# Left and right kept by pairs of channels: TensorE reads right in place at a step of 16 bytes

## Chip, cores and metric

One core of a Trainium2 chip. The metric is the device time of one execution in microseconds (us). All data are f32.

## What is computed

`x` has 384 x 384 positions of 128 channels. The first layer multiplies triangles of positions, the second gates each row:

```
z = layernorm(x)
left  = (z @ Wl + bl) * sigmoid(z @ Wlg + blg)
right = (z @ Wr + br) * sigmoid(z @ Wrg + brg)
core = einsum('bikh,bjkh->bijh', left, right)
zo = layernorm(core) @ Wout + bout
x = x + sigmoid(x @ Wg + bg) * zo
...
out = (x @ W_left + b_left + x @ W_eq + b_eq) * sum_j(x @ W_right + b_right)
out = (out * sigmoid(x @ W_gate + b_gate)) @ W_out + b_out
y = layernorm(out + x) * ln_scale + ln_bias
```

The change concerns `left`, `right` and the `einsum`: for each of the 128 channels h, a 384 x 384 by 384 x 384 product, with k summed.

## The kernel before

There are 128 partitions, and N = 384 is cut into NB = 3 blocks of 128. Each engine's instructions run in the order in which the program writes them (`seq` keeps it); the work of the stages was interleaved by hand.

**Stage 1** makes left and right. Its 144 chunks (kb, ig, c) each hold 128 positions k and XR = 8 positions i. Per position i one matmul (L372) takes the 128 x 128 columns of the normalised x as weights and `wz`, 512 columns wide, as the moving operand: left and right alternate in the first 256 results, their gates follow. For the first PLAIN = 8 chunks the weights are contiguous columns in the tile `stage`; for the rest they are taken from `columns[n][:, q, :, i]` (tile `xc`), where neighbouring columns are four f32, 16 bytes, apart. ACT makes the sigmoid (L383), DVE the product (L385), which goes to the tile `lr`, [k, h, i, s], s = 0 for left and 1 for right. So the two sides of one channel are neighbours, and a channel's G = 64 positions are a run of 512 bytes. Full `lr` tiles are stored to `lr_d` in HBM in slices of 16 channels (L357, one after each step). The last KEEP = 2 of the 18 tiles stay in SBUF (`kept`).

**Stage 2** computes core, one channel h at a time. `load_h` (L85, DMAs at L92, on SP's queue) brings left and right of a channel into `lrh`, [k, kb, i, s], in runs of 512 bytes, three channels ahead. `fill` (L576) runs on POOL: it copies the kept pieces in (L586 for left, L587 for right) and copies right out of `lrh` into the contiguous tile `rr` (L592, L593), a channel ahead. Then nine matmuls (L611), three kb by three row blocks ib, take left from `lrh` as weights, at a step of 8 bytes, and `rr` as the moving operand, 384 contiguous columns. ACT moves the result to `ct` (L620) and squares it into `sq` (L621), DVE adds both up (L622, L623), and the channel goes to `core_d` (L627), on SP's queue behind `load_h(h + 3)`.

**Stage 3** takes the variance and its root from the sums (L527 to L559; tiles `ve`, `r`, `m` of the pool `rstd`) and runs the rest row by row: L721 to L851.

Tile pools set how far each side can run ahead: two `lr` tiles, three `lrh`, two `rr`, two `ct`, one `sq`.

Of the kernel before, what the change touches and what calls it, by code (L numbers as in the profile page):

```python
# [8 lines left out]
F32 = mybir.dt.float32  # L9
# [5 lines left out]
P = 128  # L15
# [4 lines left out]
def triangle_then_gated_row_kernel(ctx: ExitStack, tc: tile.TileContext, a: dict, out: bass.AP):  # L20
# [13 lines left out]
    nc = tc.nc  # L34
    x_nat, x_tok, x_row = a["x_nat"], a["x_tok"], a["x_row"]
    NG8, C = x_nat.shape[1], x_tok.shape[2]
    N = 8 * NG8
    H = a["L0_side_b"].shape[0] // 4
    assert C == P and H == P and N % P == 0
    NB = N // P  # L40
    G = 64
    NG = N // G
    XR = 8
    KEEP = 2
# [3 lines left out]

    cpool = ctx.enter_context(tc.tile_pool(name="const", bufs=1))
    dpool = ctx.enter_context(tc.tile_pool(name="scratch", bufs=1, space=DRAM))  # L50
    lr_d = dpool.tile([NB * NG, P, H, 2 * G], F32, name="lr_d")
    core_d = dpool.tile([N, H, N], F32, name="core_d")
    rstd_d = dpool.tile([N, N], F32, name="rstd_d")
    nd_d = dpool.tile([NB * NG8, 8 * P], F32, name="nd_d")
# [1 line left out]
    def seq(ins):  # L56

        return tc.keep_in_program_order(ins)
# [19 lines left out]
    kept = {(NB - 1, ig): None for ig in range(NG - KEEP, NG)}  # L78
    end2 = ctx.enter_context(ExitStack())
    with ExitStack() as ctx2:  # L80
        lrp = ctx2.enter_context(tc.tile_pool(name="lr", bufs=2))
        inp = [ctx2.enter_context(tc.tile_pool(name="p2in", bufs=2))]
        loaded2 = {}

        def load_h(h):  # L85

            if h < H:
                t = inp[h % 3 // 2].tile([P, NB, N, 2], F32, tag="lrh", name="lrh")
                src = lr_d[:, :, h].rearrange("g p e -> p g e")
                dst = t.rearrange("p b (g i) s -> p (b g) (i s)", i=G)  # L90
                for g in slice(0, NG), slice(NG, NB * NG - KEEP):
                    seq(nc.sync.dma_start(out=dst[:, g], in_=src[:, g]))  # L92
                loaded2[h] = t

        with tc.tile_pool(name="p1w", bufs=5, side="right") as wp, \
# [6 lines left out]
            NQ = XR // 4  # L104
            AHEAD, LEAD = 4, 15
            FETCH = 6
            HS = H // 8
            loaded, normed = {}, {}
            lr, full = {}, []
            batches, at = [(n, n + 1) for n in range(PLAIN)], PLAIN  # L110
# [28 lines left out]
                seq(nc.sync.dma_start(out=t[0:1], in_=nd_d[n:n + 1, 4 * P * q:4 * P * (q + 1)]))  # L139


            stage = lrp.tile([P, H, G, 2], F32, tag="lr", name="stage").rearrange("p h i s -> p (h i s)")
            load_chunk(0, slice(0, 4))

            wst, g0, b0 = stage[:, 0:4 * H], stage[:, 4 * H:4 * H + 1], stage[:, 4 * H + 1:4 * H + 2]
# [207 lines left out]
            def store_slice():  # L353

                if full:
                    kb, ig, hs, t = full.pop(0)
                    seq(nc.sync.dma_start(  # L357
                        out=lr_d[kb * NG + ig, :, hs:hs + HS].rearrange("k h e -> k (h e)"),
                        in_=t[:, hs:hs + HS].rearrange("k h i s -> k (h i s)"),
                    ))  # L360

            def back(n, q, half, between=None):


                kb, ig, c = chunks[n]
                if c == 0 and q == 0 and half == 0:
                    lr[kb, ig] = lrp.tile([P, H, G, 2], F32, tag="lr", name="lr")
                t = lr[kb, ig]
                pr = pps.tile([P, 2, 4 * H], F32, tag="pr", name="pr")
                for r in range(2):  # L370
                    i = 2 * half + r
                    seq(nc.tensor.matmul(  # L372
                        pr[:, r, :], lhsT=columns[n][:, 4 * q + i, :] if n < PLAIN else columns[n][:, q, :, i],
                        rhs=wz, start=True, stop=True,
                    ))
                    if r == 0 and between:
                        between()
                r0 = 4 * q + 2 * half
                own, c0 = normed[n]
                rs = [terms[own][3][:, c0 + r:c0 + r + 1] for r in range(r0, r0 + 2)]  # L380
                sg = [wp.tile([P, 2 * H], F32, tag="sg", name="sg") for _ in range(2)]
                for r in range(2):
                    seq(nc.scalar.activation(sg[r], pr[:, r, 2 * H:], AF.Sigmoid, scale=rs[r]))  # L383
                for r in range(2):
                    seq(nc.vector.scalar_tensor_tensor(  # L385
                        t[:, :, c * XR + r0 + r, :],
                        pr[:, r, :2 * H].rearrange("k (h s) -> k h s", s=2),
                        rs[r],
                        sg[r].rearrange("k (h s) -> k h s", s=2),
                        ALU.mult, ALU.mult,  # L390
                    ))
                if c == G // XR - 1 and q == NQ - 1 and half == 1:
                    if (kb, ig) in kept:
                        kept[kb, ig] = t
                    else:
                        full.extend((kb, ig, hs, t) for hs in range(0, H, HS))

            steps = [(n, q) for n in range(len(chunks)) for q in range(NQ)]
            fetch = {0: [4, 5], 1: [6, 7]}
# [45 lines left out]
            for n in range(PLAIN, len(chunks)):  # L445
                k = 2 + (n - PLAIN) // 2
# [12 lines left out]
            for k, (n, q) in enumerate(steps):  # L459
# [4 lines left out]
                if k > 0:  # L464
                    more = 4 if k in (6, len(steps) - 6) else 1
# [47 lines left out]
                    late_products(m2)  # L513
                if k == len(steps) - 2 * G // 4 + 16:
                    assert not full
                    for h in range(2):
                        load_h(h)


        spool, rp = (end2.enter_context(tc.tile_pool(name=n, bufs=b, side="right", reuse_waits="tile"))  # L520
                     for n, b in (("stats", 1), ("rstd", 2)))
        roots = {}


# [1 line left out]

        def variance(b, s):  # L527
            if b not in roots:
                roots[b] = [rp.tile([P, N], F32, tag=n, name=n, bufs=c) for n, c in (("ve", NB), ("r", NB), ("m", 2))]
            ve, _, m = (w[:, s] for w in roots[b])  # L530
            if b > 0:
                seq(nc.scalar.activation(m, csum[:, b, s], AF.Square, scale=1.0 / H))
                seq(nc.scalar.activation(ve, csq[:, b, s], AF.Copy, scale=1.0 / H))
                seq(nc.gpsimd.tensor_tensor(ve, ve, m, ALU.subtract))
                seq(nc.gpsimd.tensor_scalar(ve, ve, 0.0, EPS, ALU.max, ALU.add))
                return
            seq(nc.vector.scalar_tensor_tensor(m, csum[:, b, s], 1.0 / (H * H), csum[:, b, s], ALU.mult, ALU.mult))
            seq(nc.vector.scalar_tensor_tensor(ve, csq[:, b, s], 1.0 / H, m, ALU.mult, ALU.subtract))
            seq(nc.vector.tensor_scalar(ve, ve, 0.0, EPS, ALU.max, ALU.add))
# [18 lines left out]
            seq(nc.vector.scalar_tensor_tensor(r, r, -0.5, ve, ALU.mult, ALU.mult))  # L558
            seq(nc.vector.scalar_tensor_tensor(r, r, 1.5, m, ALU.add, ALU.mult))  # L559

        with tc.tile_pool(name="p2r", bufs=2, side="right", reuse_waits="tile") as rrp, \
             tc.tile_pool(name="p2more", bufs=1, side="right", reuse_waits="tile") as more, \
             tc.tile_pool(name="p2out", bufs=2, side="right", reuse_waits="tile") as op, \
             tc.tile_pool(name="p2sq", bufs=1, side="right", reuse_waits="tile") as qp, \
             tc.tile_pool(name="p2ps", bufs=2, space=PSUM, reuse_waits="tile") as ps, \
             tc.tile_pool(name="p2one", bufs=1, space=PSUM, reuse_waits="tile") as ps1:
            csum = spool.tile([P, NB, N], F32, name="csum")
# [2 lines left out]
            seq(nc.vector.memset(csq, 0.0))  # L570

            inp.append(more)
            load_h(2)
            right = {}

            def fill(h):  # L576

                if h < H:
                    t = loaded2[h]
                    rr = right[h] = rrp.tile([P, NB, N], F32, tag="rr", name="rr")  # L580
                    i1 = G * (NG - KEEP)

                    def stay():
                        for (kb, ig), lrt in kept.items():
                            i = slice(ig * G, (ig + 1) * G)
                            seq(nc.gpsimd.tensor_copy(t[:, kb, i, 0], lrt[:, h, :, 0]))  # L586
                            seq(nc.gpsimd.tensor_copy(rr[:, kb, i], lrt[:, h, :, 1]))  # L587


                    if h > 0:  # L590
                        stay()
                    seq(nc.gpsimd.tensor_copy(rr[:, :NB - 1], t[:, :NB - 1, :, 1]))  # L592
                    seq(nc.gpsimd.tensor_copy(rr[:, NB - 1, :i1], t[:, NB - 1, :i1, 1]))  # L593
                    if h == 0:
                        stay()

            fill(0)
            for h in range(H):
                fill(h + 1)
                t, rr = loaded2.pop(h), right.pop(h)  # L600
                pc = ps.tile([P, NB, 512], F32, tag="pc", name="pc")
                banks = [pc[:, ib, :N] for ib in range(NB)]
                order = [(kb, ib) for kb in range(NB) for ib in range(NB)]
# [5 lines left out]
                    seq(nc.scalar.activation(warm, mhalf[:, 0:1], AF.Sqrt, scale=-1.0))  # L609
                for kb, ib in order:  # L610
                    seq(nc.tensor.matmul(  # L611
                        banks[ib], lhsT=t[:, kb, ib * P:(ib + 1) * P, 0], rhs=rr[:, kb],
                        start=(kb == 0), stop=(kb == NB - 1),
                    ))

                ct = op.tile([P, NB, N], F32, tag="ct", name="ct")
                sq = qp.tile([P, NB, N], F32, tag="sq", name="sq")
                to = core_d[:, h, :].rearrange("(b p) j -> p b j", p=P)
                if h < H - 1:
                    seq(nc.scalar.copy(ct, pc[:, :, :N]))  # L620
                    seq(nc.scalar.activation(sq, ct, AF.Square))  # L621
                    seq(nc.vector.tensor_add(csum, csum, ct))  # L622
                    seq(nc.vector.tensor_add(csq, csq, sq))  # L623
                    load_h(h + 3)

                    queue = nc.sync if h < H - 3 else nc.scalar
                    seq(queue.dma_start(out=to, in_=ct))  # L627
# [24 lines left out]
    with ExitStack() as ctx3:  # L652
# [49 lines left out]
        i1 = 0  # L702
# [280 lines left out]
```

## Time and profile before

| | us |
|---|---|
| median of three runs (lowest to highest) | 3155.5 (3154.95 to 3156.49) |
| the profiled execution's own time | 3154.78 |
| its span in the profile | 3152.9 |
| stage 1, to the first matmul of L611 | 1010 |
| stage 2, the matmuls of L611 | 742.9 |
| stage 3 | 1400 |
| share of 16 DMA engines busy, HBM traffic over the span | 74%, 252 GB/s |

How to read it. An f32 matmul appears as two MATMUL records on PE, each with one LDWEIGHTS record on PEld, which overlaps PE: 1152 matmuls of L611 are 2304 records. A group's row gives the line, engine, operation, what it writes and reads, its shape and count, then busy us and the mean ns of one, then the engine's idle time before it and what ended it. Records of a busy PE overlap, so busy time over count, not the mean, is the pace. The chain is the work that ended last, followed back from the end. The granted clock of TensorE is 0.999 of full speed in this execution.

### The profile page before, as it was taken

The numbers are of one execution on the slowest core, as the hardware profiler recorded it, in microseconds if no ns is written. First come the engines' busy times: TensorE is split into PE (matmuls) and PEld (weight loads), VectorE is DVE, ScalarE is ACT, GpSimd is POOL, SyncE is SP. The second block draws the span as 40 slices with busy tenths as digits, with TensorE's granted clock in tenths as the row PEclk, the third lists the DMA queues.
The fourth block names the chain that finished last, engine by engine and source line by source line (L and its number), as shares of the span: only waits on it lengthen the run. The fifth ranks groups of instructions, "written<-read, shape, count | busy, mean of one in ns | idle before, by whom it ended". The sixth has DMA issues, their size and how long they took to land.

```text
span 3152.9 us, 44536 instructions
## 1 busy us (share of the span) xinstructions
PE 3135.5 (99%) x11306; PEld 2132.8 (68%) x11306; DVE 2473.6 (78%) x7409; ACT 1808.5 (57%) x3755; POOL 2392.9 (76%) x3066
## 2 busy tenths in 40 slices
PE   9999999999999999999999999999999999999998
PEld 4777777777776666666666666677777777777776
DVE  8888888888885555555555788888888888888998
ACT  4444444444444343343433577777777777777777
POOL 6888888888886656666566587788888888888887
PEclk9999999999999999999999999999999999999999
DMA  4978878788883999999999865666666666666562
GB/s 154 340 302 304 326 279 340 281 320 299 312 304 106 282 282 283 282 284 282 284 282 283 298 231 202 220 224 221 219 220 218 221 220 219 220 220 222 210 213 109
DMA packets 509102, 797.42 MB, mean 253 GB/s; under 512 B 56689, under 2 KB 419569, under 8 KB 492466
## 3 DMA queue, kind: packets, MB, share of 16 engines
q1 hardware_dynamic: 507552, 792.61, 74.0%
q8 instruction: 94, 1.54, 0.2%
q10 hardware_dynamic: 1234, 1.77, 0.2%
q14 instruction: 158, 1.29, 0.1%
q0 software_dynamic: 64, 0.20, 0.0%
HBM read 508.14 MB, written 286.36 MB: 252 GB/s over the span
## 4 chain that ended last, share of the span: by engine, by line
PE 98%; DVE 1%; ACT 0%; issue 0%; DMA 0%; POOL 0%; POOLq 0%; DVEq 0%; ACTq 0%
PE pr L372 31%; PE pc L611 23%; PE py L781 8%; PE pr L752 8%; PE pg L769 8%; PE pl L770 8%; PE pg L721 8%; PE py L782 4%; DMA core_d<-ct 0%; PE pt L335 0%; PE pq L729 0%; ACT py L816 0%; PE pb L740 0%; POOL rs L286 0%; DVE m L547 0%
## 5 line engine op out<-in xcount | busy, mean ns | idle before, releaser
L372 PE MATMUL pr<-wz,xc 128*128 128x512 f32 x2176 | 935.1, 592 | 0.0
L372 PEld LDWEIGHTS pr<-wz,xc 128*128 128x128 f32 x2176 | 670.5, 308 | 263.9 <-POOL xc L324 1.2
L383 ACT ACTIVATE sg<-pr,rs 128x256 f32<-128x256 f32 x1152 | 483.8, 471 | 508.3 <-ACT sg L383 354.7
L611 PE MATMUL pc<-rr,lrh 128*128 128x384 f32 x2304 | 743.3, 486 | 0.4 <-DVE lr L385 0.4
L611 PEld LDWEIGHTS pc<-rr,lrh 128*128 128x128 f32 x2304 | 452.0, 196 | 291.8 <-issue 1.1
L385 DVE SCALAR_TENSOR_TENSOR lr<-pr,rs,sg 128x256 f32<-128x256 f32 x1152 | 501.7, 477 | 164.3 <-ACT sg L383 158.9
L816 ACT ACTIVATE py<-py,nm,rs 128x128 f32<-128x128 f32 x1149 | 493.1, 430 | 159.7 <-DVE u L774 80.6
L781 PEld LDWEIGHTS py<-wo,u 128*128 128x128 f32 x2304 | 376.6, 191 | 97.5
L622 DVE TENSOR_TENSOR csum<-csum,ct 128x1152 f32<-128x1152 f32 x127 | 175.0, 1378 | 332.9 <-ACT ct L620 332.9
L781 PE MATMUL py<-wo,u 128*128 128x128 f32 x2304 | 402.1, 275 | 0.0
L620 ACT COPY ct<-pc 128x1152 f32<-128x1152 f32 x127 | 142.3, 1120 | 445.2 <-PE pc L611 439.7
L743 POOL TENSOR_TENSOR cs<-ct,rt 128x384 f32<-128x384 f32 x380 | 379.7, 1000 | 8.3 <-DMA rt<-rstd_d 4.4
L851 POOL TENSOR_TENSOR yt<-yt,lnb 128x384 f32<-128x384 f32 x380 | 380.6, 1003 | 2.9 <-DVE yt L845 2.6
L324 POOL TENSOR_TENSOR xc<-xc,bc 128x512 f32<-128x512 f32 x272 | 345.8, 1271 | 24.0
L286 POOL TENSOR_TENSOR rs<-nd,mhalf 128x8 f32<-128x8 f32 (+1 forms) x145 | 236.3, 1630 | 146.8 <-ACT sg L383 107.2
L796 DVE BATCH_NORM_STATS2 st<-py 128x6 f32<-128x128 f32 x1152 | 266.0, 286 | 87.2 <-PE py L782 85.1
L592 POOL COPY rr<-lrh 128x768 f32<-128x768 f32 x128 | 190.8, 1490 | 167.2 <-DMA lrh<-lr_d 156.4
L782 PE MATMUL py<-ident,x1T 128*128 128x128 f32 x1152 | 314.0, 273 | 0.0
L752 PE MATMUL pr<-cs,wc 128*128 128x384 f32 x768 | 313.5, 490 | 0.0
L769 PE MATMUL pg<-x1T,mat_L_conv_W_gate 128*128 128x384 f32 x768 | 310.7, 486 | 0.9 <-ACT g L772 0.9
L721 PE MATMUL pg<-xt,mat_L_conv_Wg 128*128 128x384 f32 x768 | 310.7, 487 | 0.3 <-ACT ct L635 0.2
L770 PE MATMUL pl<-x1T,mat_L_conv_W_left 128*128 128x384 f32 x768 | 310.5, 486 | 0.0
(124 smaller groups left out, 4302.2 us busy)
## 6 DMA issues: line engine op xcount, KB each, us to landing
lr_d<-lr SPq DMA_DIRECT2D x128, 1024.0 KB
lrh<-lr_d SPq DMA_DIRECT2D x128, 640.0 KB
xt<-in_x_row_dram SPq DMA_DIRECT2D x96, 768.0 KB
ct<-core_d SPq DMA_DIRECT2D x95, 768.0 KB
rt<-rstd_d SPq DMA_DIRECT2D x95, 768.0 KB
out_dram<-yt SPq DMA_DIRECT2D x94, 768.0 KB
core_d<-ct SPq DMA_DIRECT2D x125, 576.0 KB
xt<-in_x_nat_dram SPq DMA_DIRECT2D x136, 512.0 KB
```

The lines of the kernel that those rows point to most:

```text
L372: seq(nc.tensor.matmul(pr[:, r, :], lhsT=columns[n][:, 4 * q + i, :] if n < PLAIN else columns[n][:, q, :, i], rhs=wz, start=True, stop=Tr ...
L383: seq(nc.scalar.activation(sg[r], pr[:, r, 2 * H:], AF.Sigmoid, scale=rs[r]))
L385: seq(nc.vector.scalar_tensor_tensor(t[:, :, c * XR + r0 + r, :], pr[:, r, :2 * H].rearrange("k (h s) -> k h s", s=2), rs[r], sg[r].rearra ...
L611: seq(nc.tensor.matmul(banks[ib], lhsT=t[:, kb, ib * P:(ib + 1) * P, 0], rhs=rr[:, kb], start=(kb == 0), stop=(kb == NB - 1),))
L721: seq(nc.tensor.matmul(pg[:, :N], lhsT=wg0, rhs=r["xT"], start=True, stop=True))
L752: seq(nc.tensor.matmul(pr[:, :N], lhsT=wc, rhs=r["cs"], start=True, stop=True))
L769: seq(nc.tensor.matmul(pg2[:, :N], lhsT=wgate, rhs=r["x1T"], start=True, stop=True))
L770: seq(nc.tensor.matmul(pl[:, :N], lhsT=wleft, rhs=r["x1T"], start=True, stop=True))
L781: seq(nc.tensor.matmul(py[:, s], lhsT=r["u"][:, s], rhs=r["wo"], start=True, stop=False))
L782: seq(nc.tensor.matmul(py[:, s], lhsT=r["x1T"][:, s], rhs=ident, start=False, stop=True, is_transpose=True))
L816: seq(nc.scalar.activation(py[:, s], py[:, s], AF.Identity, bias=bias, scale=scale))
L851: seq(engine.tensor_tensor(yt, yt, lnbb, ALU.add))
```

## The change

The two innermost sizes are regrouped: a tile holds pairs of channels, and for a position four values lie together, left and right of the even channel and left and right of the odd one. A pair's 64 positions are one run of 1 KB in `lr` and in `lr_d`. Loads are by pair and block kb (`load_block`) in place of by channel, with five buffers of [k, 384, 4], a pair's three loads placed after the second channel's matmuls. `fill`, `rr` and POOL's copies of right are gone: L611's successor takes both weights and moving operand from `lrh`, each at a step of four f32, 16 bytes. POOL copies only the kept pieces, four values at a time, once a pair (`fill_last`). `sq` and the tiles of the root share one tile, `arena`. The counts of matmuls, and what they compute, are as before.

```diff
-    lr_d = dpool.tile([NB * NG, P, H, 2 * G], F32, name="lr_d")
+    lr_d = dpool.tile([NB * NG, P, H // 2, 4 * G], F32, name="lr_d")
...
-        inp = [ctx2.enter_context(tc.tile_pool(name="p2in", bufs=2))]
+        inp = [ctx2.enter_context(tc.tile_pool(name="p2in", bufs=3))]
...
-        def load_h(h):
-
-            if h < H:
-                t = inp[h % 3 // 2].tile([P, NB, N, 2], F32, tag="lrh", name="lrh")
-                src = lr_d[:, :, h].rearrange("g p e -> p g e")
-                dst = t.rearrange("p b (g i) s -> p (b g) (i s)", i=G)
-                for g in slice(0, NG), slice(NG, NB * NG - KEEP):
-                    seq(nc.sync.dma_start(out=dst[:, g], in_=src[:, g]))
-                loaded2[h] = t
+        def load_block(n):
+
+            p, kb = divmod(n, NB)
+            if p < H // 2:
+                t = loaded2[p, kb] = inp[n % 5 // 3].tile([P, N, 4], F32, tag="lrh", name="lrh")
+                g = slice(kb * NG, (kb + 1) * NG - (KEEP if kb == NB - 1 else 0))
+                seq(nc.sync.dma_start(
+                    out=t.rearrange("p (g i) e -> p g (i e)", i=G)[:, :g.stop - g.start],
+                    in_=lr_d[g, :, p].rearrange("g p e -> p g e"),
+                ))
...
-                    lr[kb, ig] = lrp.tile([P, H, G, 2], F32, tag="lr", name="lr")
+                    lr[kb, ig] = lrp.tile([P, HP, G, 4], F32, tag="lr", name="lr")
...
-                        pr[:, r, :2 * H].rearrange("k (h s) -> k h s", s=2),
+                        pr[:, r, :2 * H].rearrange("k (h e) -> k h e", e=4),
...
+        arena = spool.tile([P, 2 + 2 * NB, N], F32, name="arena")
+        own_root = [[arena[:, n] for n in place] for place in ((0, 1, 2), (3, 5, 7), (4, 6, 2))]
...
-            def fill(h):
...
-                    seq(nc.gpsimd.tensor_copy(rr[:, :NB - 1], t[:, :NB - 1, :, 1]))
-                    seq(nc.gpsimd.tensor_copy(rr[:, NB - 1, :i1], t[:, NB - 1, :i1, 1]))
...
+            def fill_last(h):
+
+                if h < H and h % 2 == 0:
+                    for (kb, ig), lrt in kept.items():
+                        seq(nc.gpsimd.tensor_copy(loaded2[h // 2, kb][:, ig * G:(ig + 1) * G], lrt[:, h // 2]))
...
-                        banks[ib], lhsT=t[:, kb, ib * P:(ib + 1) * P, 0], rhs=rr[:, kb],
+                        banks[ib], lhsT=loaded2[h // 2, kb][:, ib * P:(ib + 1) * P, 2 * (h % 2)], rhs=loaded2[h // 2, kb][:, :, 2 * (h % 2) + 1],
...
+                if h % 2 == 1:
+                    for n in range(5, 5 + NB):
+                        load_block(h // 2 * NB + n)
+                fill_last(h + 1)
...
-                sq = qp.tile([P, NB, N], F32, tag="sq", name="sq")
+                sq = arena[:, 3:3 + NB]
```

## The prediction

> **What bounds the kernel now.** I read the shares and the chain of the page first, then its groups. Columns of a group: busy us, mean ns of one instruction, idle before it. A matmul in f32 is two MATMUL records with two weight loads (PEld LDWEIGHTS); I call each a pass.
>
> ```profile
> PE 3135.5 (99%) x11306; PEld 2132.8 (68%) x11306; DVE 2473.6 (78%) x7409; ACT 1808.5 (57%) x3755; POOL 2392.9 (76%) x3066
> ...
> PE 98%; DVE 1%; ACT 0%; issue 0%; DMA 0%; POOL 0%; POOLq 0%; DVEq 0%; ACTq 0%
> ...
> L372 PEld LDWEIGHTS pr<-wz,xc 128*128 128x128 f32 x2176 | 670.5, 308 | 263.9 <-POOL xc L324 1.2
> ...
> L611 PE MATMUL pc<-rr,lrh 128*128 128x384 f32 x2304 | 743.3, 486 | 0.4 <-DVE lr L385 0.4
> L611 PEld LDWEIGHTS pc<-rr,lrh 128*128 128x128 f32 x2304 | 452.0, 196 | 291.8 <-issue 1.1
> ...
> L592 POOL COPY rr<-lrh 128x768 f32<-128x768 f32 x128 | 190.8, 1490 | 167.2 <-DMA lrh<-lr_d 156.4
> ```
>
> TensorE is the bound everywhere: 99% busy, 98% of the chain. Stage 2, which the change rewrites, is the L611 row: 2304 passes in 743.3 us, 322.6 ns a pass, with 0.4 us of idle before them. (The mean of 486 ns is one pass from its start to its end; passes overlap, so I price by busy time over count.) The stretches by stage say the same: cut at the first and last pass of L611, that line alone:
>
> ```profile
> 1010.00:1752.90 742.90, 742.83 (x2304) 451.98 (x2304) 1.00 0.95 282
> ```
>
> (length, PE, PEld, granted clock, DMA share, GB/s). So a stage of 742.9 us has no PE gap to win, at full clock. Whatever POOL or the DMAs do less of there gains nothing; whatever a pass costs more counts 2304 times.
>
> The row that matters most comes from the weight loads split by form:
>
> ```profile
> L372 PEld LDWEIGHTS pr<-wz,xc 128*128 128x128 f32 x2176 | 670.5, 308 | 263.9 <-POOL xc L324 1.2 <-issue 0.7
> L611 PEld LDWEIGHTS pc<-rr,lrh 128*128 128x128 f32 x2304 | 452.0, 196 | 291.8 <-issue 1.1
> ...
> L372 PEld LDWEIGHTS pr<-wz,stage 128*128 128x128 f32 x128 | 22.9, 190 | 24.6 <-issue 19.4 <-ACT stage L336 3.5 <-ACT sg L383 1.7
> ```
>
> One instruction, 128 columns each, three steps between columns: 4 bytes (the first eight chunks, from stage) 190 ns; 8 bytes (lrh) 196 ns; 16 bytes (xc) 308 ns. The first and the last are the same line of code, with the same matmul beside them. TensorE's own read of SBUF in f32 is thus 118 ns dearer for 128 columns at 16 bytes, and nearly free at 8. Moving operands, in contrast, are all contiguous before: wz, rr, xt, cs, x1T. No row shows a strided one.
>
> Who waits in stage 2 (total us, times, longest), and the DMA line of the same stretch (the queue's packets, MB, share of 16 engines):
>
> ```profile
> ACT ct L620 <- PE pc L611: 432.7, 124, 3.5
> DVE csum L622 <- ACT ct L620: 328.0, 125, 3.4
> POOL rr L592 <- DMA lrh<-lr_d: 155.7, 123, 3.1
> POOL rr L587 <- PE pc L611: 120.7, 125, 2.1
> ...
> q1 hardware_dynamic: 310791, 204.84, 95.2%
> ```
>
> All wait for PE; but the DMA engines are 95% occupied, so loads have little room.
>
> **What the Trainium skill says.** "SBUF — State Buffer", section Door 1 (the note on cachelines): SBUF is read in lines of 16 bytes, at least two accesses must hit a line to absorb its latency, and an access that goes to a new line each time pays. It then says that 4 fp32 can be strided for free, which is just this change's 16 bytes. The trace sides with the first sentence and against the second: 308 ns against 190. "TensorE: Matmul & The Clock Gate", Part 2: weights and moving operand have two independent read ports. So the weight row is an analogy for the moving one, and not its measurement; that both run beside each other undisturbed agrees with L372, where 308 ns of load hide under a pass of 430 (935.1/2176). "DMA: Bandwidth & Descriptors", Specifications: 512 bytes are the least for full rate. Loads before are at just that, and 95% busy at 282 GB/s; nothing before shows what 1 KB gives.
>
> **The change part by part.**
> - *Right as moving operand in place, step 16 bytes.* Each of 384 columns now lies in its own line. Contiguous, a pass takes 322.6/384 = 0.84 ns a column. The weight load's extra at 16 bytes is 118 ns for 128 columns, 0.92 ns each: about one more such step a column. The moving read's price is not in the trace. So from both sides. Below: 0, if the moving port fetches a line in 0.84 ns or less. A gain is excluded: the columns are as many, and contiguous is the best case. Above: the weight row's whole extra, 118 x 3 = 354 ns a pass, x 2304 = 816 us. Between lies the plain doubling, 320 ns a pass (a second 0.833 ns step for 384 columns): 2304 x 320 = 737 us. I take 740: the remaining 11 ns of the 118 look like a start-up cost, which passes in a row would hide. All of it is on the path, since PE is the path.
> - *Left as weights, step 8 to 16 bytes:* from 196 to 308 ns, from the two rows. It lies beside the previous pass; 308 < 322 even if passes stay as they are, so 0. If that cover were short by 10 ns, 23 us; with doubled passes it has over 300 ns to spare.
> - *POOL copies removed:* 128 of L592 (1490 ns) and as many of L593, and four pieces of 64 a channel; in their place two copies of 256 elements a pair of channels. POOL was 449 of 724 us busy in stage 2 and released only matmuls that never waited: 0. Each new copy is about 0.5 us at L592's 1490/768 = 1.9 ns an element; PE's kb = 2 matmuls of the pair wait for it. It is queued behind nothing on POOL.
> - *Loads by block:* three DMAs a pair (512, 768, 768 KB) for four before, the same 2 MB, half the packets. They go out on SP after the pair's last matmuls release each buffer, so the store of core_d for the odd channel stands behind them on SP; ACT needs that ct buffer only two channels later: 0. With stage 2 doubled the traffic falls to about 282/2 = 141 GB/s, and nothing here is late.
> - *Stage 1:* L385 writes 4 in a row where it wrote 2, as many elements (477 ns, two for each 1.72 us of four passes); slices to lr_d remain 8 KB a partition: 0. First loads: 2 MB as before. *Arena:* sq and the roots share space, each still written before it is read on the same engines, at the seam where all wait for the last matmuls: 0, at most the seam's chain, 2 to 3 us (PE idles 0.3 us there now).
>
> Sum against the profiled execution: 3154.8 (span 3152.9 and 1.9 around it) + 740 = 3895. The median of the runs is 0.7 above that execution; I leave 3895.
>
> **The rivals.**
> - *A, doubled passes* (640 to 680 ns each): 3154.8 + 737 to 816 = 3892 to 3971; with some 15 us of slop, 3875 to 3985. For it: the weight row on the same engine, and the page's two-hit sentence.
> - *B, the moving port is quick enough: not slower.* Place: the L611 pass. Price: 0. It decides from a line fetch of at most 0.84 ns (322.6/384). Then 322 ns passes stay and only the seams move: 3150 to 3158. For it: separate ports, and "4 fp32" free. Against it: 308.
> - *C, B's port, but block loads are late.* The kb = 2 block is asked for when three matmuls of the odd channel are done, and used twelve matmuls later: 12 x 0.645 = 7.7 us. In that time: the store issue before it on SP 2.0 us (median of L627), its transfer 590 KB / 282 = 2.1, the block 524 KB / 282 = 1.9, two copies 1.0: 7.0 us. If 1 to 2 us more, x 64 pairs = 64 to 128: 3220 to 3285. Under A the deadline is 15 us and this is void.
> - *D, half a step:* a line costs 1.25 ns, +160 ns a pass: 2304 x 160 = 369 us, 3524.
> - *E, worse than twice:* the line fetch is slower than the weights' 1.7 ns, or stalls drop the granted clock. At twice A's extra: 3155 + 1480 = 4635.
>
> **How the numbers follow.** A 0.72, B 0.08, C 0.06, D 0.09, E 0.05. Predicted: A's 3895. Range: A and D, 3500 to 3985, 0.81; A's own is 3875 to 3985. The measurement tells 0.2% (6 us) from no change. Faster 0.02, out of B, whose seams can hardly give 6 us; same 0.06, the rest of B; slower 0.92, A, C, D, E.
>
> **What would show it.** A: the matmul line of stage 2 has 1475 to 1560 us busy over 2304 passes, its record grows from 486 to about 806 ns, its weight loads stand at 308 with long idle; POOL and DMA shares in stage 2 fall below half; stages 1 and 3 keep 1010 and 1400 us; granted clock stays 1.00. A pass below 340 ns says B or C: then PE idle released by POOL copies is C. A pass near 480 is D. A clock under 0.9 in stage 2 is E. It is wrong if the moving read costs nothing at 16 bytes.

## The result, and the profile after

The changed kernel takes 3982.4 us (median of four runs, 3982.0 to 3983.5) beside 3155.4 for the kernel before: 1.262 times as long (95% interval 1.260 to 1.264), +827 us. The forecast was 3895 with a range of 3500 to 3985. The direction and the place were right; the size sits at the upper edge, 2.6 us inside it.

Shares, chain and groups from the page of the changed kernel. L595 is the old L611, L374 the old L372, L581 the copies of the kept pieces:

```profile
PE 3963.3 (100%) x11306; PEld 2395.8 (60%) x11306; DVE 2403.2 (60%) x7409; ACT 1808.6 (45%) x3755; POOL 1983.1 (50%) x2426
...
PE 99%; DVE 0%; POOL 0%; ACT 0%; issue 0%; DMA 0%; SPq 0%; POOLq 0%; DVEq 0%
...
L595 PE MATMUL pc<-lrh 128*128 128x384 f32 x2304 | 1571.0, 861 | 0.5 <-DVE lr L387 0.5
L595 PEld LDWEIGHTS pc<-lrh 128*128 128x128 f32 x2304 | 715.0, 310 | 856.0 <-issue 856.0
L374 PE MATMUL pr<-wz,xc 128*128 128x512 f32 x2176 | 935.1, 592 | 0.7 <-POOL xc L326 0.7
...
L374 PEld LDWEIGHTS pr<-wz,xc 128*128 128x128 f32 x2176 | 670.5, 308 | 264.6 <-POOL xc L326 2.0
...
L581 POOL COPY lrh<-lr 128x256 f32<-128x256 f32 x128 | 47.8, 403 | 1509.5 <-issue 1386.9
```

The page's first line looks as healthy as before: PE reads 100% where it read 99% (99.5 and 99.4 with one more digit). That is the trap of a busy share. The same 2304 matmul records fill 1571.0 us where they filled 743.3, and PE still has only 0.5 us of idle ahead of them. A pass is 1571.0/2304 = 681.9 ns, against 322.6. The difference, 827.7 us, is the whole result. The weight loads stand at 310 ns, where the same step took 308 before (L372). PEld is now idle for 856 us; the profile names no releaser, but busy and idle together, 715.0 + 856.0, are just the 1571.0 us of the matmuls. L374 itself has not moved (935.1 us both times).

By stage (length, then busy us and instructions of PE, PEld, DVE, ACT, POOL, granted clock, DMA share, GB/s):

```profile
0.00:1010.00 1010.00, 1004.39 (x2390) 704.63 (x2391) 832.96 (x2861) 492.05 (x1169) 813.25 (x737) 1.00 0.78 285
1010.00:2580.00 1570.00, 1569.54 (x2304) 714.66 (x2304) 339.91 (x265) 293.85 (x262) 47.42 (x127) 1.00 0.42 134
2580.00:3981.00 1401.00, 1389.33 (x6614) 976.53 (x6613) 1230.34 (x4283) 1022.72 (x2326) 1122.42 (x1562) 1.00 0.61 214
```

Stages 1 and 3 keep their 1010 and 1400 us. Stage 2 runs at a granted clock of 1.00, so the clock isn't the cause; POOL is down to 3% and the DMAs to 42% at 134 GB/s. Every resource that the change relieves is relieved, and none of them was the bound.

### The profile page after: what moved, and what is told of

It is laid out like the page before. It is cut to its first block, busy times and chain, and to the rows that moved or that the text cites. A ratio compares the mean times of both kernels' runs of the same rounds, so it can differ in the third digit from the quotient of the medians.

```text
span 3981.7 us, 43765 instructions
## 1 busy us (share of the span) xinstructions
PE 3963.3 (100%) x11306; PEld 2395.8 (60%) x11306; DVE 2403.2 (60%) x7409; ACT 1808.6 (45%) x3755; POOL 1983.1 (50%) x2426
## 3 DMA queue, kind: packets, MB, share of 16 engines
q10 hardware_dynamic: 1234, 1.77, 0.1%
## 4 chain that ended last, share of the span: by engine, by line
PE 99%; DVE 0%; POOL 0%; ACT 0%; issue 0%; DMA 0%; SPq 0%; POOLq 0%; DVEq 0%
PE pc L595 39%; PE pr L374 24%; PE py L769 6%; PE pr L740 6%; PE pg L709 6%; PE pg L757 6%; PE pl L758 6%; PE py L770 3%; DMA stage<-in_x_nat_dram 0%; PE pq L717 0%; PE pt L337 0%; POOL rs L288 0%; DVE lr L387 0%; DVE st L265 0%; ACT py L804 0%
## 5 line engine op out<-in xcount | busy, mean ns | idle before, releaser
L595 PE MATMUL pc<-lrh 128*128 128x384 f32 x2304 | 1571.0, 861 | 0.5 <-DVE lr L387 0.5
L595 PEld LDWEIGHTS pc<-lrh 128*128 128x128 f32 x2304 | 715.0, 310 | 856.0 <-issue 856.0
L374 PE MATMUL pr<-wz,xc 128*128 128x512 f32 x2176 | 935.1, 592 | 0.7 <-POOL xc L326 0.7
L611 DVE TENSOR_TENSOR csum<-csum,ct 128x1152 f32<-128x1152 f32 x127 | 172.5, 1358 | 1225.1 <-ACT ct L609 1225.1
L374 PEld LDWEIGHTS pr<-wz,xc 128*128 128x128 f32 x2176 | 670.5, 308 | 264.6 <-POOL xc L326 2.0
L581 POOL COPY lrh<-lr 128x256 f32<-128x256 f32 x128 | 47.8, 403 | 1509.5 <-issue 1386.9
```

What stands on the lines that cost most here:

```text
L374: seq(nc.tensor.matmul(pr[:, r, :], lhsT=columns[n][:, 4 * q + i, :] if n < PLAIN else columns[n][:, q, :, i], rhs=wz, start=True, stop=Tr ...
L595: seq(nc.tensor.matmul(banks[ib], lhsT=loaded2[h // 2, kb][:, ib * P:(ib + 1) * P, 2 * (h % 2)], rhs=loaded2[h // 2, kb][:, :, 2 * (h % 2) ...
```

## The experiments

My theory, L, formed after the result: a moving operand is read line by line, 1.78 ns for each 16-byte line (681.9/384; the expectations say 1.77 or 1.76), and never faster than 0.84 ns a column. Rivals: H, only columns alone in their line pay; W, the read merely doubles to 640 ns and the strided weight loads beside it add 42; C, late blocks; and a price on the step itself.

**1. The step out, all the rest of the change in** (core is a product with other values; twelve executions).

```diff
-  rhs=loaded2[h // 2, kb][:, :, 2 * (h % 2) + 1],
+  rhs=loaded2[h // 2, kb].rearrange("p i e -> p (i e)")[:, :N],
```

> The changed kernel, all of it, but the moving operand is the first 384 contiguous values of the same tile, so core is a product with other values. It leaves only the step of the right side out. L and H: 322 ns a pass, the weights' 310 ns stay hidden, 3155. Rival C of the prediction (block loads or POOL copies late): PE idle released by POOL, 3220 to 3285. Theory W (the strided weight loads slow the matmuls beside them): above 330 ns a pass, up to 3250.

Measured: 3156.2 us, 1.000 times before (0.9991 to 1.0009). Stage 2's rows, split by form:

```profile
L595 PE MATMUL pc<-lrh 128*128 128x384 f32 x2304 | 743.4, 486 | 0.4 <-DVE lr L387 0.4
L595 PEld LDWEIGHTS pc<-lrh 128*128 128x128 f32 x2304 | 710.2, 308 | 33.8 <-issue 1.1
...
L581 POOL COPY lrh<-lr 128x256 f32<-128x256 f32 x128 | 140.8, 1126 | 607.5 <-issue 561.6 <-PE pc L595 34.2 <-DVE lr L387 11.6
```

322.7 ns a pass, though its weight loads at 308 ns fill all but 33.8 us of the stage. So pairs, blocks, placement of the loads, arena and copies cost nothing together: C is out, and so is a loss from the longer weight loads while passes stay at 322 ns. POOL's copies (L581) are not behind the loads, as C had them: each pair's first copy starts within 0.1 us of the issue of a load (1310.07 beside 1309.98 us, for one), so the two run side by side.

A stretch of 724 us inside stage 2, of this run and then of the kernel before (columns as by stage above):

```profile
1016.00:1740.00 724.00, 724.00 (x2247) 692.02 (x2245) 339.23 (x249) 285.81 (x250) 138.13 (x125) 1.00 0.88 281
```

```profile
1016.00:1740.00 724.00, 724.00 (x2247) 440.48 (x2246) 398.08 (x250) 285.45 (x250) 449.49 (x749) 1.00 0.96 282
```

PE does the same in both. The 1 KB runs and loads by block do save DMA time (a share of 0.88 beside 0.96 at the same rate), and POOL falls from 449 to 138 us; neither buys time.

**2. Left contiguous, right still at 16 bytes** (core is a product with other values; one execution).

```diff
-  lhsT=loaded2[h // 2, kb][:, ib * P:(ib + 1) * P, 2 * (h % 2)],
+  lhsT=loaded2[h // 2, kb].rearrange("p i e -> p (i e)")[:, ib * P:(ib + 1) * P],
```

> The changed kernel, but the weights are 128 contiguous values of the same tile, so core is a product with other values; the moving operand keeps its step of 16 bytes. L and H: weight loads 190 ns, passes unchanged at 682 ns, 3982. W (640 ns for a doubled read and 42 for the strided weight loads beside it): 640 ns a pass, 3982 - 97 = 3885.

Measured: 3968.7 us.

```profile
L595 PE MATMUL pc<-lrh 128*128 128x384 f32 x2304 | 1557.3, 854 | 0.4 <-DVE lr L387 0.4
L374 PE MATMUL pr<-wz,xc 128*128 128x512 f32 x2176 | 935.2, 592 | 0.1
...
L595 PEld LDWEIGHTS pc<-lrh 128*128 128x128 f32 x2304 | 478.5, 208 | 1078.6 <-issue 1078.6
```

675.9 ns a pass, 6.0 less than with strided weights: W in its size (42 ns) is out, but its sign is there, 13.7 us of the 827. That is one trace against one, but L374's row differs by only 0.1 us between the two. The weight loads missed too: 208 ns, where I expected the 190 of other contiguous ones, so the strided moving read slows them a little in turn. The moving operand alone accounts for 1557.3 - 743.3 = 814 us.

**3. The kernel before with right in place at 8 bytes**, without rr; core is the same product as before; four executions.

```diff
-  rhs=rr[:, kb],
+  rhs=t[:, kb, :, 1],
```

> The kernel before with its own layout, but right read in place from lrh at a step of 8 bytes; POOL only copies the kept pieces. A pass before takes 322.6 ns. Theory L (the moving port takes 1.77 ns for each 16-byte line it touches, 682 ns over 384 lines, and never less than 0.84 ns a column): 192 lines, 340 ns a pass, 2304 x 17.5 = +40 us, about 3195. Theory H (a line touched twice is free): 322 ns, 3155. If L holds, the weights' 196 ns at 8 bytes against 190 at 4 is the same effect (64 lines x 1.77 = 113 against 107).

Measured: 3191.8 us, 1.0115 times before (1.010 to 1.013).

```profile
L595 PE MATMUL pc<-lrh 128*128 128x384 f32 x2304 | 779.9, 499 | 0.5 <-DVE lr L385 0.5
L595 PEld LDWEIGHTS pc<-lrh 128*128 128x128 f32 x2304 | 446.9, 194 | 333.5 <-issue 1.1
```

338.5 ns a pass, where L said 340 and H 322. Two columns a line are nearly free, not free, so H is out. POOL's copy into rr, which looks like plain overhead in the profile before, buys these 36 us.

**4. Right at 12 bytes** (core is a product with other values; one execution): `rhs` takes `[:, 0:3 * N:3]` of the flat tile.

> The changed kernel, but the moving operand takes 384 values of the same tile at a step of 12 bytes, so core is a product with other values. The 384 columns touch 288 lines, in fours with 2, 1 and 1 hits. L: 288 x 1.77 = 510 ns a pass, 3982 - 2304 x 172 = 3586. H (0.936 ns extra for each of the 192 columns alone in their line): 502 ns, 3568. A theory that only a step of 16 bytes or more pays: 322 ns, 3155.

Measured: 3597.5 us.

```profile
L595 PE MATMUL pc<-lrh 128*128 128x384 f32 x2304 | 1183.7, 682 | 0.4 <-DVE lr L387 0.4
```

513.8 ns a pass, 4 above L's 510 and 12 above H's 502, too close to choose between them; experiment 3 does that. That only steps of 16 bytes and more pay is out.

**5. Three patterns that part lines from steps** (core is a product with other values; one execution each), always 384 columns: two neighbours of each of 192 positions, `[:, 0:N // 2, 0:2]`; 192 values at 32 bytes, twice over; and values from two contiguous stretches in turn (the edit puts them 3072 bytes apart, not the 1536 of the expectation).

> The changed kernel, but the moving operand takes two neighbouring values of each of 192 positions, so core is a product with other values. The positions are still 16 bytes apart, but each line is touched twice in a row: 192 lines. L (1.76 ns a line, not less than 0.84 a column): 338 ns a pass, 2304 x 338 = 779 us, 3192. A theory that a pattern whose outer step is 16 bytes pays whatever its hits: 682 ns, 3982.

> The changed kernel, but the moving operand takes 192 values at a step of 32 bytes, twice over, so core is a product with other values. 384 visits, each to another line, 192 lines in all. L, by visits: 682 ns a pass, 3982, as at 16 bytes. A theory that the price grows with the step: 1000 ns or more, above 4700. A theory that lines once read stay at hand: 340 ns, 3195.

> The changed kernel, but the moving operand takes single values from two contiguous stretches 1536 bytes apart in turn, so core is a product with other values. Every line is touched four times, but never twice running: 384 changes of line over 96 lines. L counts changes of line: 682 ns a pass, 3982. A port that holds two lines: 322 to 340 ns, 3155 to 3195.

Measured: 3201.8, 4004.2 and 3352.1 us. Their rows in that order, each from its own profile:

```profile
L595 PE MATMUL pc<-lrh 128*128 128x384 f32 x2304 | 787.7, 503 | 0.4 <-DVE lr L387 0.4
```

```profile
L595 PE MATMUL pc<-lrh 128*128 128x384 f32 x2304 | 1593.2, 871 | 0.4 <-DVE lr L387 0.4
```

```profile
L595 PE MATMUL pc<-lrh 128*128 128x384 f32 x2304 | 938.5, 571 | 0.4 <-DVE lr L387 0.4
```

The first two, 341.9 and 691.5 ns a pass, agree with L: the pattern may step by 16 bytes as long as each line serves two columns, and 32 bytes cost hardly more than 16. A line read 192 columns earlier is not at hand any more, or the second would have come near 340. The first has weights at 16 bytes beside it; its 3.4 ns over experiment 3, where they are at 8, have the sign of experiment 2's 6.0, but the layouts differ too. The third is a miss: 407.3 ns is neither 682 nor 340. Columns that change line each time, but come back to it, pay 85 ns a pass and not 359. So L holds for streams that move on from line to line, and "each change of line costs 1.77 ns" is wrong as a rule; so is the other forecast, 322 to 340 ns from a port that holds two lines. What the port keeps of a line is left open.

**6. Pairs and 1 KB runs, with the copy back**; core is the same product as before; twelve executions. `fill_last` stays, and POOL copies right of each channel into rr before its matmuls:

```diff
+  rr = right[h] = rrp.tile([P, NB, N], F32, tag="rr", name="rr")
+  for kb in range(NB):
+      if kb == NB - 1:
+          fill_last(h)
+      seq(nc.gpsimd.tensor_copy(rr[:, kb], loaded2[h // 2, kb][:, :, 2 * (h % 2) + 1]))
...
-  rhs=loaded2[h // 2, kb][:, :, 2 * (h % 2) + 1],
+  rhs=right[h][:, kb],
```

> The changed kernel with its pairs, its 1 KB runs and its loads by block, but POOL copies right of each channel into a contiguous rr again, now from a step of 16 bytes, and TensorE takes rr. L: 322 ns a pass, weights 308 hidden, and the time is before's, 3155, if POOL keeps up: 1152 values a channel in 5.8 us. At 1.9 ns a value as before it takes 2.2 us; if 16 bytes cost POOL half more, 3.3 us; both fit. The rival: the last block's copy comes too late for PE, 1 us a pair or more, 3220 and up. No theory expects it under before by more than 2 us, since PE is full there.

Measured: 3156.6 us, 1.0001 times before (0.9993 to 1.001).

```profile
L607 PE MATMUL pc<-rr,lrh 128*128 128x384 f32 x2304 | 743.6, 486 | 0.4 <-DVE lr L387 0.4
L607 PEld LDWEIGHTS pc<-rr,lrh 128*128 128x128 f32 x2304 | 710.0, 308 | 34.2 <-issue 1.1 <-POOL rr L593 0.4
```

The layout is harmless as soon as the moving operand is contiguous. It isn't free for POOL. Its copies in the stretch of stage 2 from 1016 to 1740 us, and then those of right in the same stretch before:

```profile
L593 POOL COPY rr<-lrh 128x384 f32<-128x384 f32 x374 | 506.4, 1412 | 115.4 <-DMA lrh<-lr_d 114.4 <-PE pc L607 0.9
L582 POOL COPY lrh<-lr 128x256 f32<-128x256 f32 x125 | 108.5, 903 | 0.2 <-PE pc L607 0.2
```

```profile
L592 POOL COPY rr<-lrh 128x768 f32<-128x768 f32 x125 | 187.2, 1497 | 155.7 <-DMA lrh<-lr_d 155.7
L593 POOL COPY rr<-lrh 128x256 f32<-128x256 f32 x125 | 166.1, 1329 | 0.0
```

Three copies of 1412 ns are 4.2 us a channel, where the expectation had 2.2 to 3.3; the deadline of 5.8 held. Means mix two things here: before, the same step of 8 bytes cost 1497/768 = 1.9 ns a value in L592 and 1329/256 = 5.2 in L593. The traces part them by whether DVE works beside the copy. The 83 copies from 16 bytes that no DVE instruction overlaps have a median of 891 ns. Before, the 24 such copies of L593 have a median of 412 ns for 256 values, and the only one of L592 took 886 for 768. From these two I estimate 530 ns for 384 values from 8 bytes, so the step of 16 bytes makes a copy about 1.7 times as long. With DVE beside them throughout, the copies from 16 bytes take a median of 2022 ns. POOL has 115 us left of 724, and the weight loads of L607 wait for it 0.4 us in all. No version beat the kernel before, and since PE idles only 0.4 us in its stage 2, none that leaves the passes as they are can win more than that there.

## Why the prediction was right, and where its size was off

- *What bounds the kernel:* right. PE's 743 us of stage 2 set the stage; experiment 1 relieves POOL and the DMAs and wins nothing. "All wait for PE" was too broad: the line of L592 beside it shows POOL waiting 155.7 us for loads. No matmul waited for POOL, so nothing hung on it.
- *The weight row as analogy for the moving read:* right, closer than I trusted it to be. The weights' 118 ns for 128 columns, times three, gave 354 ns a pass; the moving operand alone pays 675.9 - 322.6 = 353.3 (experiment 2). The steps at 8 bytes agree too: 6 ns for 128 weight columns, 15.9 for 384 moving ones. The Trainium skill's "SBUF — State Buffer", section Door 1, has the two-hit sentence nearly right (338.5 ns with two columns a line, 681.9 with one, 322.6 with four). Its "4 fp32", read as a step that costs nothing, does not hold here: 2.1 times as long for the moving pass, 308 ns beside 190 for a weight load.
- *The term that was mis-sized:* I took 320 ns, a second step of 0.833 ns a column (the trace's own pace was 0.840), and held the weight row's other 34 for a start-up cost that passes in a row would hide. It isn't one: it grows with the columns (353.3/384 = 0.920 ns each, where 118/128 = 0.922). Worth 2304 x 33.3 = 77 us. Nothing in the profile said that a read must take a whole number of steps; the bound from the row was the better value. That the forecast range held is in part luck: the pass of 681.9 ns lies above A's 640 to 680, its 1571.0 us above A's 1475 to 1560 and its record of 861 ns above 806. The time is inside 3985 only by the 15 us of slop added to 3971.
- *Left as weights, 0 with doubled passes:* wrong by 6.0 ns a pass, 13.7 us. I reasoned that over 300 ns of cover leave nothing to pay. With contiguous passes that is so, at a cover of 15 ns even (322.7 - 308, experiment 1); beside a strided moving read it is not, and that both reads run "beside each other undisturbed" failed in both directions (6.0 ns a pass; 208 ns a weight load beside 190). The two terms, 77 + 14, make 91 us; 3895 missed by 87, the 737 having been rounded up to 740.
- *POOL, loads by block, stage 1, arena at 0:* right (experiment 1; 1.000 with its interval within 0.1%). Each kept copy took 403 ns where I put 0.5 us, but 1126 in experiment 1, beside passes of 322 ns: I had priced it from L592's 1.9 ns a value alone, when L593 took 1316 ns for 256. It cost no time, since no matmul waited for a copy.
- *Rivals:* B and C fell with the 682 ns pass, C also on its own ground in experiment 1, where passes are 322 ns and no block is late. With copies of 1.1 us in place of 0.5 C's own sum would have passed its deadline of 7.7 us, and still PE did not wait, as copies and load run side by side. D (480 ns) and E (twice A's extra, or a lower clock) are not seen.

## What to carry to other kernels

Where the trace has a row of TensorE that already reads with the step, price a new strided operand from it, and take the measured extra per column whole. Here that held from weights to a moving operand, at one shape each. In f32 keep the moving operand at two or more columns, read in a row, to each 16-byte line: one column a line made a pass 2.1 times as long, while the copy that avoids it ran on POOL under PE's work and added no time. When the bound engine reads a layout, first ask what the new layout does to its own reads, and only then what it saves the engines that wait.

## What the runs showed that I had not expected

- The price follows the reads of new lines: 96 take 322.6 ns a pass (bound by the columns), 192 take 338.5 and 341.9, 288 take 513.8, 384 take 681.9 and, at 32 bytes, 691.5: 1.76 to 1.80 ns each from 192 up.
- Beside a moving operand at 16 bytes, strided weight loads add 6.0 ns a pass (681.9 beside 675.9); beside a contiguous one they add nothing (322.7 beside 322.6).
- What DVE does beside a POOL copy goes with a larger difference than the copy's step: 384 values from 16 bytes took 891 ns with DVE idle and 2022 with DVE at work throughout, medians of experiment 6.
- Two contiguous stretches read in turn cost 407.3 ns, 26% over one stretch, though both touch 96 lines.
